# The end of the GIN layer: transpose mode for the features, and six PSUM buffers in turn

## The chip, the cores and the metric

The kernel runs on one core of a Trainium2 chip. A core has TensorE (matrix products, written to the accumulation memory PSUM), VectorE, ScalarE and GpSimd, and SyncE, which here only starts transfers. Each engine works through its own queue of instructions in order and waits at semaphores for the others. In the profile they are PE (and PEld for its weight loads), DVE, ACT, POOL and SP. The metric is the device time of one execution in microseconds (us).

## The reference

The reference is a stack of four graph layers over 3125 nodes with 128 features and 100,000 edges. Each layer is added to its input and the sum is normalised over the features of each node:

```python
x = _layernorm(x + _L0_gnn_ref(...), axis=-1)   # three GCN layers
x = _layernorm(x + _L1_gnn_ref(...), axis=-1)   # linear, summed over edges
x = _layernorm(x + _L2_gnn_ref(...), axis=-1)   # GIN
x = _layernorm(x + _L3_gnn_ref(...), axis=-1)   # two relational layers, 8 relations
```

The third, GIN, is the one that matters here:

```python
out = (1.0 + eps) * x + aggr
h = jax.nn.relu(_batchnorm(out @ W1 + b1, g1, beta1))
h = jax.nn.relu(_batchnorm(h @ W2 + b2, g2, beta2))
```

The batch normalisation needs the mean and variance of a feature over all nodes; the layer normalisation that follows needs those of a node over all features.

## The kernel before, in words

**Tiling.** The nodes are 25 blocks of 128 (`NB`), `xa` holds the current features in SBUF with nodes on the partitions, 128 x 25 x 128 float32. Most loops go over `CH`, seven chunks of 4, 3, 4, 3, 4, 3 and 4 blocks. The kernel first turns the edge list into dense adjacency blocks and per-relation count blocks (up to line 468), then runs GCN (`product`), the second layer and GIN (`product_t`), then the relational layers.

**The end of GIN.** `linear` and `batchnorm_relu` work with features on the partitions, because the batch statistics run over nodes. So their result `y2` lies transposed. The last loop of that part (lines 702 to 708) goes over the chunks. For each block it lets TensorE multiply `y2` by the identity `ident`, which transposes it into PSUM (line 706), and adds the residual by multiplying the identity with `xa` into the same PSUM columns (line 707). `normalise` with `shared=True` then takes the layer norm of a chunk out of PSUM: statistics per block on DVE (lines 123 and 124), a square root on ACT (126), reciprocal and the negated scaled mean on DVE (127, 130), and the scaling itself, even blocks on ACT (134) and odd blocks on DVE (137), written back into `xa`.

**Buffers.** The PSUM pool `f_ps` has three tags, `mi`, `acc` and `bld`, with two buffers each, and the loop takes `bld`. In this stretch of the program the other two serve earlier parts of GIN: `acc` the edge sums, `mi` the output of `linear`.

**What follows.** `x3` is `xa` under another name. A new SBUF pool `f_rel` reuses the memory of the pool in which `y2` lay, and a new PSUM pool `f_psr` reuses all of `f_ps`. Line 718 loads a weight matrix; `split2` (735 on ACT, 736 on DVE) splits `x3` in two parts for the relation product; `store3` (744 and 746 on ACT, 745 and 747 on DVE) splits it in three bfloat16 parts in a tile `t` with two buffers, and line 748 stores each chunk to the DRAM table `xt_d` through SP's queue. The relation product (`relation`) loads count blocks as bytes (758, SP's queue, six buffers), casts them on ACT (766) or DVE (768) into three buffers and multiplies (771), ten matmuls to a cast. The remaining blocks of nodes are not dense: `gathered` lets POOL gather rows of `xt_d` (805), DVE builds one-hot matrices (797), and TensorE multiplies (813). POOL cannot start before all of `xt_d` is stored. `linear1` then transposes `x3` (845), copies it (846), and applies the weights.

**What sets the order.** The kernel is written without semaphores; a scheduler that takes the program, its data dependences and the pools' buffers fixes the order of each engine's queue when the kernel is built. Instructions of a later part can therefore stand ahead of those of an earlier one, and the order can change where only a buffer name was edited.

Of the kernel before, what the change touches and what calls it, by code (L numbers as in the profile page):

```python
# [8 lines left out]
F32 = mybir.dt.float32  # L9
# [12 lines left out]
P = 128  # L22
# [23 lines left out]
def cols(m0, nb):  # L46
    return slice(m0 * P, (m0 + nb) * P)
# [7 lines left out]
CH = ((0, 4), (4, 3), (7, 4), (11, 3), (14, 4), (18, 3), (21, 4))  # L55
# [17 lines left out]
def listed(ctx: ExitStack, tc: tile.TileContext, p: dict, out: bass.AP, bad):  # L73


    nc = tc.nc
# [4 lines left out]
    ident = const.tile([P, P], F32, name="ident")  # L81
# [36 lines left out]
    def normalise(y, v, nb, shared=False):  # L118

        st = small.tile([P, 4, 6], F32, name="st")  # L120
        mv = small.tile([P, 4, 2], F32, name="mv")
        for i in range(nb):
            nc.vector.bn_stats(st[:, i, :], v[:, i, :])
            nc.vector.bn_aggr(mv[:, i, :], st[:, i, :])
        rs = small.tile([P, 4], F32, name="rs")
        nc.scalar.activation(rs[:, :nb], mv[:, :nb, 1], AF.Sqrt, bias=eps_ln, scale=1.0)
        nc.vector.reciprocal(rs[:, :nb], rs[:, :nb])
        if shared:
            ng = small.tile([P, 4], F32, name="ng")
            nc.vector.scalar_tensor_tensor(ng[:, :nb], mv[:, :nb, 0], -1.0, rs[:, :nb],  # L130
                                           op0=OP.mult, op1=OP.mult)
        for i in range(nb):
            if shared and i % 2 == 0:
                nc.scalar.activation(y[:, i, :], v[:, i, :], AF.Identity, bias=ng[:, i : i + 1],
                                     scale=rs[:, i : i + 1])
                continue
            nc.vector.tensor_scalar(
                y[:, i, :], v[:, i, :], mv[:, i, 0:1], rs[:, i : i + 1],
                op0=OP.subtract, op1=OP.mult,
            )  # L140
# [4 lines left out]
    def blocks(ap):  # L145
        return ap.rearrange("p (b c) -> p b c", c=P)

    with ExitStack() as lists, tc.tile_pool(name="f_ps", bufs=1, space=PSUM) as psum:
# [17 lines left out]
        with tc.tile_pool(name="f_t1", bufs=1) as t1:  # L166
# [24 lines left out]
            t = psum.tile([P, 512], F32, name="mi", tag="mi", bufs=2)  # L191
# [114 lines left out]
            for g in range(2):  # L306
                t = psum.tile([P, 512], F32, name="mi", tag="mi", bufs=2)
# [23 lines left out]
            t = psum.tile([P, 512], F32, name="mi", tag="mi", bufs=2)  # L331
# [5 lines left out]
            t = psum.tile([P, 512], F32, name="mi", tag="mi", bufs=2)  # L337
# [132 lines left out]
        with ExitStack() as stage:  # L470
# [165 lines left out]
            t = psum.tile([P, 512], F32, name="mi", tag="mi", bufs=2)  # L636
# [40 lines left out]
            def batchnorm_relu(y, i):  # L677

                _, g, beta = c2[i]
                ends = [(a, min(a + 512, N)) for a in range(0, N, 512)]  # L680
                st = small.tile([P, len(ends), 6], F32, name="bst")
                for j, (a, b) in enumerate(ends):
                    nc.vector.bn_stats(st[:, j, :], y[:, a:b])
                mv = small.tile([P, 2], F32, name="bmv")
                nc.vector.bn_aggr(mv, st)
                s = small.tile([P, 2], F32, name="bsc")
                nc.scalar.activation(s[:, 0:1], mv[:, 1:2], AF.Sqrt, bias=eps_ln, scale=1.0)
                nc.vector.reciprocal(s[:, 0:1], s[:, 0:1])
                nc.vector.tensor_mul(s[:, 0:1], s[:, 0:1], g)
                nc.vector.tensor_mul(s[:, 1:2], mv[:, 0:1], s[:, 0:1])  # L690
                nc.vector.tensor_sub(s[:, 1:2], beta, s[:, 1:2])
                for m0, nb in CH:
                    c = cols(m0, nb)
                    nc.scalar.activation(y[:, c], y[:, c], AF.Relu, bias=s[:, 1:2], scale=s[:, 0:1])
# [3 lines left out]
            y2 = nd.tile([P, NP], F32, name="y2", tag="halves", bufs=2)  # L698
            for m0, nb in CH:
                linear(y2, 1, y1[:, cols(m0, nb)], m0, nb)  # L700
            batchnorm_relu(y2, 1)
            for m0, nb in CH:
                t = psum.tile([P, 512], F32, name="bld", tag="bld", bufs=2)
                for i in range(nb):
                    o = t[:, cols(i, 1)]
                    nc.tensor.matmul(o, y2[:, cols(m0 + i, 1)], ident, start=True, stop=False)
                    nc.tensor.matmul(o, ident, xa[:, m0 + i, :], start=False, stop=True)
                normalise(xa[:, m0 : m0 + nb, :], blocks(t), nb, True)

# [4 lines left out]
    with tc.tile_pool(name="f_rel", bufs=1) as rp, tc.tile_pool(  # L714
        name="f_psr", bufs=1, space=PSUM
# [36 lines left out]
        def relation(r, m0, nb, pieces, work, rate, casts):  # L752

            acc = psum.tile([P, 512], F32, name="acc", tag="acc", bufs=2)
            w = nb * P
            for g in range(5):
                m8 = rp.tile([P, 4, 5, P], U8, name="m8", bufs=6)
                nc.sync.dma_start(
                    m8[:, :nb].rearrange("p b k d -> p b (k d)"),
                    rel[r][m0 : m0 + nb, :, 5 * g : 5 * g + 5].rearrange("b p k d -> p b (k d)"),  # L760
                )
                m = rp.tile([P, 5, 4 * P + 8], F32R, name="m", bufs=3)
                v = m[:, :, :w].rearrange("p k (b d) -> p k b d", d=P)
                src = m8[:, :nb].rearrange("p b k d -> p k b d")
                if casts[g]:
                    nc.scalar.copy(v, src)  # L766
                else:
                    nc.vector.tensor_copy(v, src)  # L768
                for k in range(5):
                    for i, x in enumerate(pieces):  # L770
                        nc.tensor.matmul(  # L771
                            acc[:, :w], x[:, 5 * g + k, :],
                            m[:, k, :w],
                            start=(g == 0 and k == 0 and i == 0), stop=(g == 4 and k == 4 and i == 1),
                        )
                ahead[0] += rate
                while ahead[0] >= 1.0:
                    next(work, None)
                    ahead[0] -= 1.0
            return acc[:, :w]  # L780
# [42 lines left out]
        with tc.tile_pool(name="f_z", bufs=1) as zp:  # L823
# [57 lines left out]
            for m0, nb in DENSE:  # L881
                z = zp.tile([P, R, 512], F32, name="z", bufs=2)
                for r in range(R):
                    inv = load_inv(r, m0, nb)
                    acc = relation(r, m0, nb, xs, work, 2.2, (0, 1, 0, 1, 0))
# [5 lines left out]
        with tc.tile_pool(name="f_hr", bufs=1) as hp:  # L891
# [15 lines left out]
            for m0, nb in CH:  # L907
                o = psum.tile([P, 512], F32, name="mi", tag="mi", bufs=2)
                for a in range(2):
                    nc.tensor.matmul(o[:, : nb * P], root2[:, a, :], hT[:, a, cols(m0, nb)],  # L910
                                     start=(a == 0), stop=(a == 1))
# [28 lines left out]
            for r in range(R):  # L940
                nxt = None
                for i, (m0, nb) in enumerate(DENSE):
                    inv = load_inv(r, m0, nb)
                    acc = relation(r, m0, nb, hr, work, 2.2, (1, 1, 1, 1, 1))
# [3 lines left out]
                    c = cols(m0, nb)  # L948
# [586 lines left out]
@with_exitstack  # L1535
def gnn_kernel(ctx: ExitStack, tc: tile.TileContext, p: dict, out: bass.AP):
    bad = ctx.enter_context(tc.tile_pool(name="flag", bufs=1)).tile([P, 1], I32, name="bad")
    listed(tc, p, out, bad)
    rv = tc.nc.values_load(bad[0:1, 0:1], min_val=0, max_val=1)
    with tc.If(rv > 0):  # L1540
        general(tc, p, out)
# [32 lines left out]
```

## Time and profile before

| | before |
|---|---|
| median of 3 runs | 2251.15 us (2241.75 to 2253.26) |
| the profiled execution, its own time | 2257.92 us |
| its span, first to last instruction | 2256.1 us |
| mean granted TensorE clock | 0.921 |
| busy: PE / DVE / ACT / POOL | 1932.3 / 1271.3 / 1058.1 / 903.2 us |
| line 706, first and last start | 943.5 to 968.1 us |
| first matmul of the relation product (771) | 977.1 us |
| first gather of the relation stage (805) | 1006.6 us |

A busy share is an average over stages with different limits. The changed loop takes up some 25 us of the span, so the views to read are those of that window: what each engine waits for there, and when the work that follows begins. The clock is the share of full speed that TensorE was granted. A line such as `[2.85 <-DVE xa L137]` at the end of a row says that the engine stood idle for 2.85 us before it, until DVE's work on line 137 released it.

### The profile page before, as it was taken

To read this page: it belongs to the slowest core of one execution; us is meant where nothing else is said; L and a number is where in the kernel's file an instruction comes from. 1 tells how busy PE (TensorE), PEld (TensorE's weight loads), DVE (VectorE), ACT (ScalarE), POOL (GpSimd) and SP (SyncE) were. 2 spreads that over 40 slices of the span, in tenths; PEclk is the share of its full clock that TensorE was granted. 3 is DMA by queue.
4 is the path that set the end of the run, shared out by engine and by line. 5 is a ranking of instruction groups with operands and counts; after the bars stand their busy time and mean duration, and the time that the engine had idled before them with its cause. 6 is when DMAs were issued, how large, how long until landed. Compare 5 with 4: busy or idle time off the path is not lost.

```text
span 2256.1 us, 31992 instructions
## 1 busy us (share of the span) xinstructions
PE 1932.3 (86%) x12201; PEld 1394.4 (62%) x12201; DVE 1271.3 (56%) x2303; ACT 1058.1 (47%) x1151; POOL 903.2 (40%) x898
## 2 busy tenths in 40 slices
PE   1667769999999699778998999999878899888984
PEld 1445536666665588555776667567536777767763
DVE  4888889999996563363443445344236434334423
ACT  1666644544442465541231333232227667666761
POOL 3222121121120000017747357437524766666664
PEclk9776679999999899888998999999989999999996
DMA  3444466788787788075655567456538877777762
GB/s 91 182 175 165 178 194 210 264 291 271 261 270 244 244 262 243 20 206 137 192 155 160 155 179 204 129 157 180 140 102 256 231 207 226 208 215 225 209 172 71
DMA packets 384636, 433.06 MB, mean 192 GB/s; under 512 B 28731, under 2 KB 350301, under 8 KB 384472
## 3 DMA queue, kind: packets, MB, share of 16 engines
q1 hardware_dynamic: 314318, 278.95, 40.3%
q0 software_dynamic: 45920, 119.66, 17.9%
q10 hardware_dynamic: 24234, 32.31, 5.0%
q8 instruction: 97, 1.59, 0.3%
q14 instruction: 67, 0.55, 0.1%
HBM read 319.22 MB, written 111.58 MB: 191 GB/s over the span
## 4 chain that ended last, share of the span: by engine, by line
PE 59%; DVE 17%; issue 7%; DMA 7%; ACT 4%; POOL 3%; another core or an unknown queue 2%; ACTq 0%; DVEq 0%; SPq 0%; POOLq 0%
PE acc L771 25%; PE ga L813 8%; PE acc L534 7%; PE acc L569 6%; PE mi L861 4%; PE mi L851 4%; DMA g<-dsf,irow 3%; DVE lo L161 2%; DVE rhq L161 2%; PE bld L448 2%; ACT m L766 2%; DVE hi L161 2%; DVE rlo L161 1%; POOL gx L805 1%
## 5 line engine op out<-in xcount | busy, mean ns | idle before, releaser
L771 PE MATMUL acc<-m,hilo 128*128 128x384 f32 (+1 forms) x3200 | 780.2, 387 | 50.5 <-issue 35.3
L771 PEld LDWEIGHTS acc<-m,hilo 128*128 128x128 f32 x3200 | 582.1, 195 | 139.6 <-issue 62.0
L766 ACT CAST m<-m 128x2560 fp32r<-128x2560 uint8 (+1 forms) x224 | 455.4, 2061 | 449.4 <-PE ga L813 121.9
L805 POOL DMA_INDIRECT gx<-xt_d,gsrc x355 | 391.3, 1102 | 566.0 <-DMA inv<-inv_d 306.5
L805 POOL DMA_INDIRECT gx<-ht_d,gsrc x355 | 362.5, 1021 | 220.5 <-issue 79.3
L534 PE MATMUL acc<-m,parts 128*128 128x512 bf16 (+1 forms) x1575 | 334.6, 359 | 11.6 <-DMA r_L_gnn_g<-in_L_gnn_g 10.5
L813 PE MATMUL ga<-oh,gx 128*128 128x192 bf16 (+1 forms) x2442 | 266.4, 246 | 63.4 <-issue 35.3
L813 PEld LDWEIGHTS <-gx 128*128 128x128 bf16 x2442 | 178.6, 100 | 157.2 <-issue 124.7
L797 DVE TENSOR_TENSOR oh<-iota,gkey 128x768 bf16<-128x768 bf16 (+1 forms) x188 | 100.1, 533 | 270.6 <-PE ga L813 128.0
L534 PEld LDWEIGHTS <-parts 128*128 128x128 bf16 x1575 | 152.9, 98 | 135.5 <-issue 13.9
L768 DVE CAST m<-m 128x2560 fp32r<-128x2560 uint8 (+1 forms) x96 | 152.0, 1584 | 115.6 <-issue 36.4
L455 ACT CAST rb<-bld 128x800 uint16<-128x800 f32 x179 | 143.7, 828 | 125.8 <-PE bld L448 120.7
L462 POOL DMA_DIRECT2D rel<-rb x112 | 64.4, 583 | 286.9 <-ACT rb L455 182.8
L569 PE MATMUL acc<-mf,halves 128*128 128x512 f32 (+1 forms) x700 | 154.2, 378 | 18.0 <-ACT mf L566 17.8
L569 PEld LDWEIGHTS acc<-mf,halves 128*128 128x128 f32 x700 | 128.0, 190 | 38.3 <-issue 18.7
L161 DVE TENSOR_TENSOR lo<-iota,kT 128x2048 bf16<-128x2048 bf16 x100 | 122.0, 1220 | 1.5 <-PE bld L271 1.5
L271 PE MATMUL bld<-hi,lo 128*128 128x50 bf16 x1600 | 75.8, 202 | 41.1 <-DVE hi L161 25.9
L566 ACT CAST mf<-m 128x2560 fp32r<-128x2560 bf16 (+1 forms) x42 | 88.2, 2102 | 48.1 <-PE acc L569 38.6
L448 PE MATMUL bld<-rhq,rlo 128*128 128x200 bf16 x896 | 107.7, 253 | 1.7 <-DVE rb L457 1.0
L745 DVE TENSOR_TENSOR e<-mi,t 128x512 f32<-128x512 f32 x50 | 34.3, 687 | 129.9 <-ACT t L744 125.7
L271 PEld LDWEIGHTS <-lo 128*128 128x128 bf16 x1600 | 64.9, 108 | 66.5 <-DVE hi L161 25.8
L448 PEld LDWEIGHTS <-rlo 128*128 128x128 bf16 x896 | 82.9, 98 | 36.5 <-issue 8.3
(216 smaller groups left out, 2137.2 us busy)
## 6 DMA issues: line engine op xcount, KB each, us to landing
m<-rel SPq DMA_DIRECT2D x160, 320.0 KB
rel<-rb POOLq DMA_DIRECT2D x112, 400.0 KB
m<-adj SPq DMA_DIRECT2D x60, 640.0 KB
m<-rel SPq DMA_DIRECT2D x160, 240.0 KB
m<-adj_t SPq DMA_DIRECT2D x40, 640.0 KB
m<-adj SPq DMA_DIRECT2D x45, 480.0 KB
adj_t<-at SPq DMA_DIRECT2D x25, 800.0 KB
adj<-av SPq DMA_DIRECT2D x25, 800.0 KB
```

Of the source, the lines that this page charges most:

```text
L161: nc.vector.tensor_tensor(o, (iota2 if of is None else of)[:, None, :width, :].to_broadcast([P, PU // 2, width, 2]), k[:, :, None, :].to_b ...
L271: nc.tensor.matmul(pt[:, j, : 2 * NB], lo[:, j // 2, :, j % 2], hi[:, j // 2, :, j % 2], start=True, stop=True)
L448: nc.tensor.matmul(pt[:, k, : R * NB], lo[:, j // 2, :, j % 2], hq[:, j // 2, :, j % 2], start=True, stop=True)
L455: nc.scalar.copy(o, src)
L534: nc.tensor.matmul(o, x[:, k, :], m(k - k0), start=(k == 0 and i == 0), stop=(k == NB - 1 and i == 2))
L569: nc.tensor.matmul(acc[:, :w], x[:, 5 * g + k, :], mf[:, k, :w], start=(g == 0 and k == 0 and i == 0), stop=(more is None and g == 4 and k ...
L766: nc.scalar.copy(v, src)
L768: nc.vector.tensor_copy(v, src)
L771: nc.tensor.matmul(acc[:, :w], x[:, 5 * g + k, :], m[:, k, :w], start=(g == 0 and k == 0 and i == 0), stop=(g == 4 and k == 4 and i == 1),)
L797: nc.vector.tensor_tensor(oh[:, : nt // 2], iota2[:, None, : GW * R, :].to_broadcast([P, nt // 2, GW * R, 2]), gkey[:, g, t : t + nt].rear ...
L805: nc.gpsimd.indirect_dma_start(out=gx.rearrange("p i c -> p (i c)"), out_offset=None, in_=table[:], in_offset=bass.IndirectOffsetOnAxis(ap ...
L813: nc.tensor.matmul(acc[:, a:z], gx[:, i, :], oh[:, t % 4 // 2, a - c0 : z - c0, t % 2], start=(a // 512 not in seen), stop=(t == GT[g] - 1 ...
```

## The change

The seven chunks take their PSUM tile from the tags `bld`, `mi` and `acc` in turn, each with two buffers, where all took `bld`. The product of `y2` with the identity is issued in TensorE's transpose mode, `is_transpose=True`; the addition of the residual remains an ordinary matmul that accumulates on it.

```diff
-            for m0, nb in CH:
-                t = psum.tile([P, 512], F32, name="bld", tag="bld", bufs=2)
+            for c, (m0, nb) in enumerate(CH):
+                bank = ("bld", "mi", "acc")[c % 3]
+                t = psum.tile([P, 512], F32, name=bank, tag=bank, bufs=2)
                 for i in range(nb):
                     o = t[:, cols(i, 1)]
-                    nc.tensor.matmul(o, y2[:, cols(m0 + i, 1)], ident, start=True, stop=False)
+                    nc.tensor.matmul(o, y2[:, cols(m0 + i, 1)], ident, start=True, stop=False, is_transpose=True)
                     nc.tensor.matmul(o, ident, xa[:, m0 + i, :], start=False, stop=True)
                 normalise(xa[:, m0 : m0 + nb, :], blocks(t), nb, True)
```

In the program as built, TensorE issues the chunks in the same order as before. In the queues of DVE, ACT and SP the instructions of neighbouring chunks and of the parts that follow are interleaved differently: on ACT, line 718's load and two of line 744's copies stand between the scalings of chunks 2 and 3 and those after, and the first four transposes of line 845 with their copy (846) stand ahead of the relation product's first matmul; before, they stood at the start of `linear1`, behind the products of the first chunk.

## The prediction

> **What bounds the kernel now.** I read the table by stretches first (its columns are us, then busy us and count for PE, its weight loads, DVE, ACT and POOL, then granted clock, DMA share, GB/s). From 943 to 977 us, where the changed loop lies, nothing is near full, and POOL has not begun:
>
> ```profile
> 943.00:977.00 34.00, 16.93 (x100) 16.06 (x100) 19.83 (x87) 18.39 (x39) 0.00 (x0) 0.71 0.24 65
> 977.00:1010.00 33.00, 30.11 (x120) 23.87 (x120) 23.64 (x25) 18.16 (x17) 2.84 (x3) 0.93 0.87 260
> 1010.00:1100.00 90.00, 76.45 (x412) 55.27 (x413) 31.44 (x30) 18.65 (x8) 66.10 (x62) 0.87 0.58 156
> ```
>
> So this is a chain of waits. The view of the tile `bld` names both sides, TensorE waiting for the last reader of a buffer and VectorE waiting for the last matmul of a chunk:
>
> ```profile
> L706 PE MATMUL bld<-ident,y x50: 274/304/582, 943.5 to 968.1; 128*128 128x128 f32 x50
>   DVE xa L137: 20.1, 10
>   PE bld L707: 9.7, 4
> ```
>
> The timeline shows the turn-taking. Two chunks fill both buffers, TensorE stops until L137 has read the first, and VectorE then stops until it is refilled:
>
> ```profile
> 951.33 0.80 PE L706 MATMUL bld<-ident,y 128*128 128x128 f32 x2 [2.85 <-DVE xa L137]
> 954.76 0.50 DVE L123 BATCH_NORM_STATS2 st<-bld 128x6 f32<-128x128 f32 x2 [3.13 <-PE bld L707]
> 961.01 0.50 DVE L123 BATCH_NORM_STATS2 st<-bld 128x6 f32<-128x128 f32 x2 [1.79 <-PE bld L707]
> 968.62 0.17 DVE L833 MEMSET hT<- 128x128 f32 x1 [3.16 <-PE bld L706]
> 977.07 30.11 PE L771 MATMUL acc<-m,hilo 128*128 128x512 f32 x120 [8.11 <-issue]
> 1006.55 1.04 POOL L805 DMA_INDIRECT gx<-xt_d,gsrc  x1 [306.55 <-DMA inv<-inv_d]
> 1010.33 0.43 PE L813 MATMUL ga<-oh,gx 128*128 128x192 bf16 x3 [3.15 <-DMA gx<-xt_d,gsrc]
> ```
>
> The last three lines are the stage's two exits. TensorE begins the relation product at 977.07. POOL's first gather starts at 1006.55, after the last of seven xt_d stores was issued at 1002.58. TensorE finishes its 120 matmuls and waits 3.15 us for that gather. In order of time the chain holds the xt_d stores from 977.59, then gathers to about 1027, then mostly TensorE. Downstream is therefore as early as these two exits are.
>
> **What the Trainium skill says.** "TensorE: Matmul & The Clock Gate", section Terms, calls transpose mode 4 times faster for FP32. The trace shows two: L706 leaves 50 matmul records for 25 blocks, while the existing transposes of L845 leave 25 for 25 and four start 0.44 us after one another's begin, 0.11 us each, one pass. The trace decides. Its section Part 4: PE-mode transpose says transposes do not count as busy for the clock gate in the same way; no run shows that yet. "PSUM — Partial Sum Buffer", The four PSUM rules, says that an fp32 transpose sets the bits that let the next matmul add, so L707 can go on adding. Its section on bank collisions says that two engines must not touch one bank at once. The trace agrees: within a chunk L134 (0.46 us) and L137 (0.41) alternate, the next starting 0.03 to 0.10 us after the other's end.
>
> **Transposes.** Before, a block costs four passes: 0.85 us in slow clock (944.72 to 945.57), 0.445 warm (959.36 to 959.81), so 0.213 and 0.111 a pass. After, three. Removed: 25 passes, 2.8 us warm to 5.4 cold. With two buffers only the first chunk of each of four turns is on the path: 4 passes each, three cold and one warm, 3 x 0.85 + 0.44 = 3.0 us.
>
> **Six buffers.** In the built order TensorE issues chunks 0 to 5 without a buffer wait, and chunk 6 waits for chunk 0's readers. From 943.46, cold until about 947.0 as before, 16.6 passes fit; the other 46.4 of 63 take 5.2 us: 952.2. Chunk 0's last L137 ends near 951.2 by the walk below, so chunk 6 runs 952.2 to 953.6 (before: 965.2 to 968.6).
>
> VectorE is then the stage's engine. The first statistics start at 943.46 + 12 x 0.213 + 0.15 = 946.2 (946.88 before). From there its queue holds, by start-to-start times of before: 25 statistics and aggregates, 0.19 + 0.09, 7.0; seven times L127 and L130, 1.1; eleven L137 at 0.34, 3.7; and ahead of the first relation cast L833, two L745, six L736 and two L747, 5.4; the cast itself 1.76. Sum 19.0. Walking both queues in the built order leaves 1.8 us of waiting, mostly the sqrt round trips: cast done 967.0, against a relation start of 977.07: **10.0 us**. The cross-check is the waits that go: 3.13 + 1.79 + 3.16 + 0.40, plus 0.7 earlier start and a 0.5 us one-hot moved behind, 9.7.
>
> **What moves with it.** The order changes on ACT, too. L718's DMA, which waits for chunk 6's last L706 because it reuses that memory, now stands ahead of the scaling of chunks 3 to 6. Behind it hang L134, L126, then VectorE's L137. By the walk ACT gets there at 954.2, TensorE is done at 953.5: 0.7 us of cover. SP's relation loads are freed by the same L706: 968.60 becomes about 953.6. Before, the six loads took 969.5 to 976.9 at about 1.05 us each, the first done about 3.1 after issue; after, first done 956.7, needed at 965.2, so hidden by 8.5 us. Load 6 waits for load 1's semaphore, 956.7, hidden. The four L845 transposes and the x3t copy (0.6 us ACT) go ahead of the relation product; ACT waits for a store there anyway. That takes 0.44 us from TensorE near 1120.
>
> The gather's start must be followed through stores. Two `t` buffers make each pair of stores wait for the pair before. Before: issues 977.59, 987.22, 994.84, 1002.58; landings 5.4, 3.9, 4.9, about 4. After: the first L747 ends 964.8, store 0 lands near 968.9 (no seventh load ahead); L744/745 to 970.4; the ACT cast 970.5 to 972.9, L746 to 973.4; the VectorE cast (TensorE's second group done 972.7) to 974.5, L747: store 2 at 975.1. Landing 979.0, ACT's cast to 980.0, L744, L745, cast to 983.5, L747: store 4 at 984.2. Landing 988.5, L744 to L747, SP passing load 17 at 989.3: store 6 at 991.5. Landing 4: gather near 995.4, **11.1 us** earlier than 1006.55. TensorE's 120 matmuls end near 997.2 and the first gathered data come 3.8 after the gather: resume 999.2 against 1010.33, 11.1. POOL gathers one tile per 1.25 us and idled until then, so nothing holds it back.
>
> Sum: 11.1 + 0.4 = **11.5 us**. The profiled execution took 2257.92 us (span 2256.1, 1.8 around it): 2246.4, ratio 0.9949. On the median 2251.15: **2239.7**.
>
> **Unknown ends.** A transposing pass cannot be below nothing; if it still takes two passes, the same walk gives a cast end of 969.1, 2.1 us lost. The clock: if transposes keep TensorE cold throughout, chunk 5 ends at 956.9, chunk 6 at 959.5, L718 blocks ACT for 5.3 us, cast done 972.2: a gain near 5 to 7 us. I take warm-up as before, since two of three passes stay ordinary matmuls.
>
> **Rivals.** (1) Cold TensorE, as just priced: about 2245. For it: that section of the skill, and a loop already at 0.71 clock; against: no idle turn of 2.9 us is left before chunk 6. (2) The store chain eats the gain: every other store sits on SP behind relation loads that wait for casts that wait for TensorE groups. If landings stay at 5.4 us and casts slip between each pair, 2 to 3 us a pair, the gather gains 2 to 4 us: about 2249. For it: the landing was 5.43 with loads ahead; against: TensorE's groups are 10 us earlier themselves. (3) It ends slower: the relation stages get a lower clock. TensorE holds 59% of the chain, some 1330 us, at mean clock 0.921; each 0.01 costs about 14.5 us. It cancels the gain at 0.913 and passes +0.5% at 0.905: about 2263. For it: the windows from 1010 on already vary from 0.87 to 1.00 and the three times spread over 11.5 us; against: the work there is the same. (4) The change does not do what it says, buffers still in turn of two: only 3.0 us, 2248; against: the built order shows no buffer wait before chunk 6.
>
> **Chances and range.** Half a percent, 11.3 us, is about what a measurement of this kernel can tell from no change, and my sum lies on it. Full carry-through 0.62 (about two thirds of it above 11.3, counting 3 us of unmodelled shorter waits on the gather up to 1027); cold 0.12, nearly all within, a tenth above by spread; stores 0.09 and (4) 0.04, within; slower clock 0.13, most of it past +0.5%. That is faster 0.45, same 0.44, slower 0.11. The stretch 1007 to 1027 holds about 8 us of TensorE idle under the gather, so errors of the first case lean to more gain; I move 0.05 to faster. The range takes the cold and store ends with the runs' own spread: 2229 to 2255; the likeliest case alone 2231 to 2246.
>
> **What would show it.** L706 with 25 records; no wait on L137 but at chunk 6; VectorE's idle under `bld` near 4 us instead of 9.7; relation product at 966 to 968; gather at 994 to 997; L718 not waiting past 954.5. Wrong if the clock in the loop stays near 0.5, ACT stands at L718, the store issues are not about 10 us earlier, or the clock after 1010 changes the total.

## The result, and the profile after

The change makes the kernel faster by two thirds of a percent: 2233.12 us median of 6 executions (2229.74 to 2234.57) against 2248.19 us (2241.75 to 2253.26) for the kernel before, a ratio of 0.9933 with a 95% interval of 0.9911 to 0.9954. The forecast was 2239.7 us, a ratio of 0.9949, in a range of 2229 to 2255. Two later timings of the same kernel gave 0.9931 (0.9905 to 0.9956) and 0.9953 (0.9939 to 0.9967); the forecast lies in all three intervals.

The line numbers after 702 are one higher in the changed kernel: 706 and 707 become 707 and 708, 771 becomes 772, 805 becomes 806. Its profiled execution took 2231.44 us with a span of 2229.5, and reached the changed loop 8.8 us sooner, at 934.63 us in place of 943.46, though nothing before the loop had changed. Two executions of the kernel before differ by as much as 6.7 us at that place, so times below are counted from TensorE's first matmul of the loop, and the 8.8 us are taken as scatter. These first matmuls, before and changed:

```profile
943.46 0.49 PE L706 MATMUL bld<-ident,y 128*128 128x128 f32 x2 [4.01 <-ACT y L694]
934.63 0.33 PE L707 MATMUL bld<-ident,y 128*128 128x128 f32 x1 [4.01 <-ACT y L694]
```

The table by stretches of the changed kernel, with the stretches moved by 8.8 us to match those of before (columns as there):

```profile
934.20:968.20 34.00, 22.00 (x116) 19.26 (x117) 27.33 (x98) 23.88 (x46) 0.00 (x0) 0.75 0.54 154
968.20:1001.20 33.00, 26.98 (x123) 20.00 (x122) 15.60 (x16) 12.38 (x10) 11.29 (x12) 0.95 0.72 207
1001.20:1091.20 90.00, 79.58 (x444) 60.05 (x443) 36.96 (x35) 23.34 (x10) 67.39 (x60) 0.91 0.62 166
```

VectorE's 19.8 busy us of the first stretch are now 27.3, with work that used to come later, and POOL has its first 12 instructions in the second stretch in place of 3. The view of the tile `bld` of the changed kernel:

```profile
L707 PE MATMUL bld<-ident,y x11: 272/273/421, 934.6 to 944.3; 128*128 128x128 f32 x11
  PE bld L708: 4.0, 2
```

The other 14 transposes are in `mi` and `acc`, 25 records in all in place of 50. The 20.1 us that the view of before gives for L137 count TensorE's matmuls (8.6) and their weight loads (9.1) apart, and 2.4 us of ScalarE; for TensorE they are three waits of 2.85 us. These are gone: the only wait left in the loop is the first, for the input (4.01 us, on line 694). The timeline of the changed kernel, the lines that answer to those of before:

```profile
937.08 0.49 DVE L123 BATCH_NORM_STATS2 st<-bld 128x6 f32<-128x128 f32 x2 [3.41 <-PE bld L708]
938.86 0.30 DVE L123 BATCH_NORM_STATS2 st<-mi 128x6 f32<-128x128 f32 x1 [0.68 <-PE mi L708]
940.19 0.30 DVE L123 BATCH_NORM_STATS2 st<-acc 128x6 f32<-128x128 f32 x1 [0.21 <-PE acc L708]
957.46 30.38 PE L772 MATMUL acc<-m,hilo 128*128 128x512 f32 x120 [1.56 <-DVE m L769]
986.56 1.05 POOL L806 DMA_INDIRECT gx<-xt_d,gsrc  x1 [293.54 <-DMA inv<-inv_d]
991.01 0.43 PE L814 MATMUL ga<-oh,gx 128*128 128x192 bf16 x3 [3.18 <-DMA gx<-xt_d,gsrc]
```

VectorE waits 0.68 and 0.21 us for chunks 1 and 2, then never again for TensorE. What releases the relation product is now VectorE's cast (L769), no longer the last L137. The product starts 957.46 - 934.63 = 22.8 us after the loop's start, where it was 33.6, and the gather 51.9, where it was 63.1. TensorE's wait for the gather did not change, 3.18 us after 3.15.

### The profile page after: what moved, and what is told of

It reads as the page before. It is cut to its first block, busy times and chain, and to the rows that moved or that the text cites. A ratio compares the mean times of both kernels' runs of the same rounds, so it can differ in the third digit from the quotient of the medians.

```text
span 2229.5 us, 31941 instructions
## 1 busy us (share of the span) xinstructions
PE 1911.2 (86%) x12176; PEld 1382.8 (62%) x12176; DVE 1269.3 (57%) x2303; ACT 1056.7 (47%) x1151; POOL 900.9 (40%) x898
## 4 chain that ended last, share of the span: by engine, by line
PE 58%; DVE 17%; DMA 8%; issue 7%; ACT 4%; another core or an unknown queue 3%; POOL 2%; ACTq 0%; SPq 0%; DVEq 0%; POOLq 0%
PE acc L772 24%; PE ga L814 7%; PE acc L534 7%; PE acc L569 6%; PE mi L852 4%; PE mi L862 3%; DVE lo L161 2%; DMA g<-dsf,irow 2%; PE bld L448 2%; DVE rhq L161 2%; ACT m L767 2%; DVE hi L161 2%; DVE rlo L161 1%; DMA back<-ht_d 1%
## 5 line engine op out<-in xcount | busy, mean ns | idle before, releaser
L772 PEld LDWEIGHTS acc<-m,hilo 128*128 128x128 f32 x3200 | 580.4, 194 | 132.3 <-issue 53.1
L534 PE MATMUL acc<-m,parts 128*128 128x512 bf16 (+1 forms) x1575 | 333.7, 358 | 11.6 <-DMA r_L_gnn_g<-in_L_gnn_g 10.5
L769 DVE CAST m<-m 128x2560 fp32r<-128x2560 uint8 (+1 forms) x96 | 151.9, 1584 | 115.8 <-PE ga L814 32.2
```

The costliest lines, as they stand in the source:

```text
L534: nc.tensor.matmul(o, x[:, k, :], m(k - k0), start=(k == 0 and i == 0), stop=(k == NB - 1 and i == 2))
L772: nc.tensor.matmul(acc[:, :w], x[:, 5 * g + k, :], m[:, k, :w], start=(g == 0 and k == 0 and i == 0), stop=(g == 4 and k == 4 and i == 1),)
```

## The experiments

The theory: two buffers made TensorE and VectorE take turns; six let VectorE set the pace; the time won there moves both exits, the relation product and the gather, and is carried to the end unchanged. The rivals: transpose mode is the larger part; the later stages add a gain of their own; only one exit counts. Two of the chips here run the kernel before in some 2155 us and the others in some 2249, so a run is compared with the kernel before on its own chip. On the two faster chips the kernel before was timed but not profiled; the early-turn kernel, which ran on one of them and has the loop of the kernel before, stands in for it there. The table has, for each kernel's profiled execution, us from the loop's first matmul, read from the start times of the relation product, the first gather and the span's end, and the ratio of times with its interval.

| kernel | relation product | first gather | end | ratio to before |
|---|---|---|---|---|
| before | 33.6 | 63.1 | 1312.7 | |
| before again | 33.6 | 63.4 | 1316.1 | 1.000 (0.998 to 1.002) |
| changed | 22.8 | 51.9 | 1294.9 | 0.9933 (0.9911 to 0.9954) |
| changed, third | 22.8 | 53.1 | 1305.8 | 0.9953 (0.9939 to 0.9967) |
| four loop buffers | 22.9 | 51.7 | 1300.4 | 0.9959 (0.9933 to 0.9985) |
| scaling on ScalarE | 18.6 | 55.5 | 1303.1 | 0.9954 (0.9937 to 0.9971) |
| four store buffers | 24.1 | 42.8 | 1290.2 | 0.9911 (0.9882 to 0.9940) |
| four store buffers again | 25.1 | 44.1 | 1287.5 | 0.9896 (0.9866 to 0.9927) |
| four store buffers, scaling on ScalarE | 18.8 | 46.4 | 1290.1 | 0.9894 (0.9861 to 0.9927) |
| *on the chips of 2155 us:* | | | | |
| early turn only | 34.4 | 65.3 | 1216.7 | 1.0006 (0.9994 to 1.0019) |
| transpose only | 34.1 | 64.2 | 1211.2 | 0.9989 (0.9975 to 1.0004) |
| transpose, kept busy | 31.0 | 61.1 | 1214.6 | 0.9989 (0.9977 to 1.0001) |
| buffers only | 25.6 | 52.2 | 1204.9 | 0.9944 (0.9924 to 0.9965) |
| changed, again | 22.8 | 52.9 | 1206.4 | 0.9931 (0.9905 to 0.9956) |

**Transpose mode alone.**

```diff
-                bank = ("bld", "mi", "acc")[c % 3]
+                bank = "bld"
```

> Transpose mode alone, all seven chunks in the two bld buffers as before. If the loop is bound by the turns of TensorE and VectorE (my theory), only the first chunk of each of four turns is on the path: 3.0 us in the loop, from TensorE's first transposing matmul to the first matmul of the relation product 30.6 us in place of 33.6, ratio near 0.9987. If TensorE's passes set the loop, all 25 passes count, 2.8 to 5.4 us, and the waits on L137 (20.1 us) shrink. Rival on the stages after it: the transposes of x3 stay where they were before, so if their early place makes the later gain, this kernel keeps none of that part.

Measured: 0.9989, an interval that holds 1, and the loop was not shortened at all, 34.1 us where 30.6 was forecast. The windows of the loop's four turns, first of the kernel before, then of this one (columns as above; the granted clock is the third number from the end; this kernel's first window opens 0.7 us before its first matmul):

```profile
943.40:951.33 7.93, 5.02 (x28) 4.83 (x28) 3.52 (x21) 5.69 (x12) 0.00 (x0) 0.75 0.01 2
951.33:958.92 7.59, 4.73 (x28) 4.54 (x29) 3.82 (x22) 2.28 (x6) 0.00 (x0) 0.81 0.00 0
958.92:965.17 6.25, 3.39 (x29) 3.21 (x29) 3.82 (x22) 2.28 (x6) 0.00 (x0) 0.94 0.00 0
965.17:977.10 11.93, 3.82 (x17) 3.55 (x17) 8.77 (x25) 7.84 (x15) 0.00 (x0) 0.50 0.67 185
```

```profile
937.50:945.85 8.35, 4.19 (x21) 4.00 (x22) 3.70 (x21) 6.79 (x13) 0.00 (x0) 0.76 0.00 0
945.85:953.19 7.34, 3.85 (x21) 3.66 (x21) 3.69 (x21) 2.20 (x6) 0.00 (x0) 0.73 0.01 2
953.19:961.43 8.24, 4.74 (x22) 4.45 (x22) 3.77 (x21) 2.20 (x6) 0.00 (x0) 0.50 0.00 0
961.43:972.40 10.97, 2.86 (x13) 2.59 (x13) 8.48 (x24) 7.39 (x14) 0.00 (x0) 0.50 0.73 200
```

The third turn has a quarter fewer passes and takes longer, 8.24 us in place of 6.25, at a clock of 0.50 where the kernel before had 0.94. The two kernels were profiled on chips of different speed, but that is not the reason: the early-turn kernel, on the same chip as this one, has the third turn of the kernel before:

```profile
953.84:960.09 6.25, 3.39 (x29) 3.20 (x29) 3.81 (x22) 2.28 (x6) 0.00 (x0) 0.94 0.00 0
```

The waits for a buffer grew as well, from 2.85 to 3.43 and 3.49 us, and end with ScalarE's L134 in place of VectorE's L137, since the order of scaling differs. Two causes were open, the clock and these waits, and the next kernel tells them apart.

**Transpose mode with TensorE kept busy.** On top of the edit above, it computes something more: nine products that nothing reads.

```diff
                     nc.tensor.matmul(o, ident, xa[:, m0 + i, :], start=False, stop=True)
+                if c % 2 == 1:
+                    idle = psum.tile([P, 512], F32, name="mi", tag="mi", bufs=2)
+                    for _ in range(3):
+                        nc.tensor.matmul(idle, ident, y2[:, : 4 * P], start=True, stop=True)
                 normalise(xa[:, m0 : m0 + nb, :], blocks(t), nb, True)
```

> Transpose mode with the two bld buffers, and nine products of 512 columns that nothing reads, put where TensorE waits for a buffer: four behind the first turn, five behind the second. ScalarE's and VectorE's queues stand as in transpose mode alone, which kept the loop at 34.1 us with its third turn at half clock (0.64 us a block). If the lower clock took the saving away, the third turn runs at 0.33 us a block and is 1.2 us shorter at least in what VectorE waits for, loop 32 to 33 us. If it was the longer wait for the scaling in the new order, the loop stays at 34 us although the clock is up.

Its windows over the same four turns (the first opens 0.8 us before the first matmul), and the wait before its fourth turn:

```profile
937.40:945.85 8.45, 7.61 (x29) 5.36 (x29) 3.71 (x21) 6.91 (x13) 0.00 (x0) 0.80 0.01 2
945.85:952.53 6.68, 6.68 (x32) 4.24 (x32) 3.66 (x21) 2.20 (x6) 0.00 (x0) 1.00 0.00 0
952.53:958.52 5.99, 2.50 (x23) 2.30 (x22) 3.66 (x21) 2.20 (x6) 0.00 (x0) 1.00 0.00 0
958.52:969.30 10.78, 2.66 (x13) 2.40 (x13) 8.47 (x24) 7.37 (x14) 0.00 (x0) 0.51 0.73 203
958.52 0.33 PE L707 MATMUL bld<-ident,y 128*128 128x128 f32 x1 [3.49 <-ACT xa L134]
```

With useless work added, the third turn runs at full clock and takes 5.99 us, and the loop 31.0 us in place of 34.1, more than the 32 to 33 expected. The queues of VectorE, ScalarE and SyncE hold the same instructions in the same order, and the wait of 3.49 us is still there before the fourth turn, so the lower clock had taken the saving. What lowered it is less sure: each of the two kernels was profiled once, and no run separates the fewer passes, the longer gap and transpose mode itself. In the total 3 us are near the limit of what was measured: the ratio is 0.9989 again.

**Buffers alone.**

```diff
-                    nc.tensor.matmul(o, y2[:, cols(m0 + i, 1)], ident, start=True, stop=False, is_transpose=True)
+                    nc.tensor.matmul(o, y2[:, cols(m0 + i, 1)], ident, start=True, stop=False)
```

> Six buffers in turn alone, the features multiplied by the identity in the ordinary mode. My theory: VectorE sets the loop as soon as the buffers let TensorE run ahead; four passes a block in place of three delay the first statistics and the last L706 by some 1 us each, cast done 2.1 us later than in the full change: loop to relation product near 25 us in place of 33.6, gain 8 to 9 us plus what the stages after it add, ratio near 0.996. If transpose mode were the larger part: less than 4 us.

```profile
938.74 0.49 PE L707 MATMUL bld<-ident,y 128*128 128x128 f32 x2 [4.01 <-ACT y L694]
964.31 27.26 PE L772 MATMUL acc<-m,hilo 128*128 128x512 f32 x105 [12.51 <-issue]
990.97 1.43 POOL L806 DMA_INDIRECT gx<-xt_d,gsrc  x1 [295.92 <-DMA m<-rel]
```

Measured: 25.6 us (964.31 - 938.74), close to the 25 expected, and a ratio of 0.9944. The buffers bring most of the change. Transpose mode then takes 2.8 us more off the start of the relation product (22.8), but not off the gather: 52.2 us with the buffers alone, 51.9 to 53.1 with both. In the totals the two can't be told apart (2144.39 and 2141.95 us on one chip).

**Four buffers in the loop.**

```diff
-                bank = ("bld", "mi", "acc")[c % 3]
+                bank = ("bld", "mi")[c % 2]
```

> Transpose mode with four buffers, bld and mi in turn. My theory: VectorE is the loop's engine once TensorE can run ahead by two chunks, so TensorE waits some 1 us for chunk 4's buffer and nothing is lost: 23 to 24 us to the relation product (22.9 with six), ratio 0.993 to 0.9945. If six are needed: waits on L137 of 3 us or more come back and the relation product is at 26 us or later.

Measured: TensorE waits on L137 again, 0.96 and 0.94 us, and nothing behind it notices: 22.9 us and 51.7 us. Four buffers are enough here. The ratio, 0.9959, lies above the 0.993 to 0.9945 expected, but its interval (0.9933 to 0.9985) overlaps all three of the changed kernel.

**The early transposes alone.** The kernel before, with the transposes of the first chunk of `x3` and their copy written ahead of the relation product, which gives the stores the paired order of the changed kernel.

```diff
-            def linear1(z, m0, nb):
-                w = min(nb * P, HL - m0 * P)
+            def turned(m0, nb):
                 x3t = zp.tile([P, 512], F32, name="x3t", bufs=1)
                 t = psum.tile([P, 512], F32, name="mi", tag="mi", bufs=2)
                 for i in range(nb):
                     nc.tensor.transpose(t[:, cols(i, 1)], x3[:, m0 + i, :], ident)
                 nc.scalar.copy(x3t[:, : nb * P], t[:, : nb * P])
+                return x3t
+
+            head = turned(*CH[0])
+
+            def linear1(z, m0, nb):
+                w = min(nb * P, HL - m0 * P)
+                x3t = turned(m0, nb) if m0 else head
```

> The kernel before, with one of the change's side effects alone: the transposes of the first chunk of x3 and their copy stand ahead of the relation product; GIN's end is as before. Plain shift: 0.44 us from TensorE, ratio 0.9990 to 1.0005. Rival: the changed order of stores and casts that comes with it (xt_d stores in pairs) is worth 3 us or more, ratio 0.9985 or less, with the first gather 1 us or more earlier relative to the first relation matmul.

Measured: 1.0006 (0.9994 to 1.0019), and the gather came later after the relation product, not earlier: 30.9 us in place of 29.5. This side effect is worth nothing that can be measured; the 0.4 us of the sum are neither confirmed nor refuted.

**The two kernels again.** Both without an edit.

> The kernel before once more, timed against itself and profiled on the chip of the others. Ratio 1.000, and from TensorE's first matmul in the loop 33.6 us to the relation product, 63 us to the first gather, 1205 to 1220 us to the end if the chip is like that of the runs before it. What differs is the scatter that the comparison of any two profiles carries.

> The changed kernel once more, for a second execution with a profile and a time on the chip of the others. Theory of a plain shift: 10.8 us at the first relation matmul and 11.2 at the first gather stay 11 to 12 us to the end, and the 17.7 us that the first pair of profiles shows from the loop to the end is partly scatter of one execution (expect 10 to 14 here). Rival: the later 3 to 7 us come again at the same places (200 gathers on, and in the second relational layer), 16 to 18 us from the loop to the end. Ratio 0.993 to 0.995 in both.

> The changed kernel once more, beside the two that follow on the same chip. Plain shift: 23 us from the loop's first matmul to the relation product, 52 to 53 to the first gather; from the first gather to the end the same as the kernel before within 5 us. Ratio 0.993 to 0.995.

The places in the loop come again to within 0.1 us for the relation product and 1.2 us for the gather. The later stretch does not. From the first gather to the end, the kernel before takes 1312.7 - 63.1 = 1249.6 and 1252.7 us; the changed one 1243.0 and 1305.8 - 53.1 = 1252.7. On the faster chip the changed kernel takes 1153.5, the early-turn kernel, which is like the one before, 1151.4. So the 17.7 us from the loop to the end that the first two profiles differ by hold some 6 of scatter, and no later stage has been shown to add a gain. The third timing's ratio, 0.9953, fell just outside the 0.993 to 0.995 expected of it.

**Scaling on ScalarE.** This takes VectorE's 11 L137 off the loop.

```diff
-            if shared and i % 2 == 0:
+            if shared:
```

> The changed kernel with all the scaling of this loop on ScalarE (25 L134 in place of 14, no L137 in the loop). My theory, VectorE sets the loop: 11 x 0.34 = 3.7 us leave it and the turns within a bank go, ScalarE takes 11 x 0.35 = 3.9 more of its own 24 us: relation product 2 to 3 us earlier (20 to 21 us after the loop's first matmul), ratio near 0.992. If ScalarE is as near its limit: no change or 1 to 2 us later.

Measured: the relation product starts 4.2 us earlier, more than the 2 to 3 expected. That fits a loop that VectorE paces, but the edit also ends the turns of the two engines within a bank, and no run tells these two apart. The gather starts 2.4 to 3.6 us later than in the changed kernel, and the ratio, 0.9954 where 0.992 was expected, is no better. Moving one exit forward and the other back gained nothing.

**Four buffers for the stored split.**

```diff
-            t = rp.tile([P, 4, 3, D], BF, name="t3", bufs=2)
+            t = rp.tile([P, 4, 3, D], BF, name="t3", bufs=4)
```

> The changed kernel with four buffers in place of two for the three-part split that is stored to xt_d, so that no pair of stores waits for the pair before. My theory says that the first gather, not the first relation matmul, decides what the rest gets: then the gather starts 8 us or more earlier (about 44 us after the loop's first matmul in place of 52), TensorE's wait for it goes, and 4 to 8 us come on top of the full change, ratio against before near 0.990. Rival, the relation product's start decides: the casts stand behind the stores' splits on both engines, it starts 1 to 2 us later, and the total is that of the full change or 1 us more.

> Four buffers for the stored split, once more. If the first gather decides: gather at 43 us after the loop's first matmul, relation product at 24, and 4 us or more less than the changed kernel on the same chip (ratio 0.990 to 0.992). If the 4 us of the first time were scatter: within 2 us of the changed kernel.

SP's queue, first of the changed kernel, then of the second profile of this one (start, length, count of transfers; only the stores' lines are shown, the loads between them left out):

```profile
955.34 1.06 SPq L749 DMA_DIRECT2D xt_d<-t  x2
967.05 0.91 SPq L749 DMA_DIRECT2D xt_d<-t  x2
975.69 1.78 SPq L749 DMA_DIRECT2D xt_d<-t  x2
982.78 0.36 SPq L749 DMA_DIRECT2D xt_d<-t  x1
```

```profile
958.20 1.19 SPq L749 DMA_DIRECT2D xt_d<-t  x2
962.92 0.91 SPq L749 DMA_DIRECT2D xt_d<-t  x2
968.49 0.36 SPq L749 DMA_DIRECT2D xt_d<-t  x1
972.15 0.45 SPq L749 DMA_DIRECT2D xt_d<-t  x1
975.01 0.36 SPq L749 DMA_DIRECT2D xt_d<-t  x1
```

The same profile's first matmul of the loop, relation product and first gather:

```profile
936.67 0.47 PE L707 MATMUL bld<-ident,y 128*128 128x128 f32 x1 [4.01 <-ACT y L694]
961.75 4.42 PE L772 MATMUL acc<-m,hilo 128*128 128x512 f32 x10 [2.02 <-DVE m L769]
980.77 1.05 POOL L806 DMA_INDIRECT gx<-xt_d,gsrc  x1 [288.12 <-DMA inv<-inv_d]
```

From the first store to the last, 27.4 us became 16.8. The gather starts at 42.8 and 44.1 us, the relation product 1.3 and 2.3 us later than in the changed kernel, and the kernel is faster: 2226.29 us against 2237.43 for the changed one on the same chip, and the two intervals of the ratio to before do not touch (0.9866 to 0.9927, 0.9939 to 0.9967). This version beats both kernels, and the exit that counts, by all that was measured, is the gather. The table shows it: on the slower chips the nine profiles take 1243 to 1253 us from the first gather to the end, a spread of 10 us, but 1262 to 1284 us, a spread of 22, from the relation product. The traces show it early in that stretch. The 50th of 355 gathers starts 134.6 and 134.9 us after the loop's first matmul in the two profiles of the kernel before, 123.5 and 125.1 in the changed kernel, 125.7 with the scaling on ScalarE, 114.6 and 116.6 here: what the gather won is still there, and the earlier product of the kernel with the scaling on ScalarE is not.

Two things keep this from being a test of the gather alone. The built order also differs: TensorE's queue has the first gathered products behind 70 relation matmuls, not 120, and TensorE's wait for the first gather, expected to go, is 3.13 us as before. And the tile `t` serves the later stores to `ht_d` too; but as the time from the gather to the end, 1247.4 and 1243.4 us, is within that of the other kernels, no gain from these is seen.

> Four buffers for the stored split and all scaling of this loop on ScalarE. With six buffers for the loop alone the scaling on ScalarE brought the relation product 4.2 us forward and the gather 3.6 us back, because ScalarE also serves the stored split. If the gather decides, this is no better than four store buffers alone: gather at 43 to 46 us, relation product at 20, ratio 0.990 to 0.993. If both exits count alike: 2 us or more below it, ratio 0.989.

With the scaling on ScalarE added to it (both edits above), the relation product starts 6.3 us earlier again, the gather 2.3 us later (46.4), and the total stays, 2226.87 us. That fits the same reading but does not prove it: the intervals of the two ratios (0.9861 to 0.9927, 0.9866 to 0.9927) are wider than what is to be told apart.

## Why the prediction was right, point by point

**Six buffers** was right in its mechanism and nearly in its size. Predicted from the loop's first matmul, and measured: first statistics 2.7 and 2.45 us; chunk 6 begins at 8.7 and 8.7; relation loads issued at 10.1 and 10.0; cast done 23.5 and 22.8; so 10.0 us were forecast for the relation product and 10.8 came. VectorE's idle time under TensorE was to be near 4 us and is 3.41 + 0.68 + 0.21 = 4.3.

**What moves with it** held. L719's load stands ahead of the scaling and cost nothing: ACT came to it at 10.2 us, when L707's last pass was just done, and the copy behind it waited 0.12 us. The chain of stores was forecast at 21.4, 31.6, 40.7 and 48.0 us and measured at 20.7, 32.4, 41.1 and 48.2; the gather at 51.9 and 51.9, 11.1 us and 11.2. TensorE resumed at 56.4 where 55.7 was forecast, 10.5 us earlier in place of 11.1.

**Transposes** is the step that failed, in its claim for two buffers: "3 x 0.85 + 0.44 = 3.0 us" took the clock of each turn as given. The third turn lost it, and nothing was left. With TensorE kept busy the loop takes 31.0 us, 2.6 less than the 33.6 of the kernel before, and that with a clock of 1.00 in the second turn where the kernel before had 0.81; so the 3.0 us are near in size, but no run shows them at an equal clock. In the changed kernel this did not matter, as TensorE runs its loop through without a pause; there the transposes took 2.8 us off the start of the relation product, where the walk had 2.1. The statement of the Trainium skill, "TensorE: Matmul & The Clock Gate", Part 4: PE-mode transpose, that transposes do not count as busy for the clock gate in the same way, which carried rival 1, did not decide here: with a third of the passes in transpose mode the loop went from 0.213 to 0.111 us a pass some 4 us after its start, as before. No run had transposes alone.

**The sum** added 0.4 us for the early transposes, for which no run shows a gain. And the prediction did not say which of the two exits counts: both were forecast to come 10 to 11 us earlier, so the result could not show it. There was luck in that. The later kernels speak for the gather: product starts 4 and 6 us earlier, with the gather 2 to 4 us later, brought no total that could be told from the one without, and a gather about 9 us earlier, with the product 1 to 2 us later, took 11 us off. The sum was right because it followed the gather. Its 11.5 us compare with 15.1 (10.3 to 20.0 by the interval), 14.9 and, the narrowest, 10.6 us by the ratio's 0.0047 (7.4 to 13.7).

**The rivals.** Cold TensorE, the store chain and buffers still in turn of two are excluded by the profile. A lower clock did not come, 0.928 against 0.921. The reason given for leaning to more gain, shorter waits on the gather, was wrong: the first wait was 3.18 us, and 4.47 in the third profile, and in 20 us from just behind the gather's start, TensorE was busy for 12.60 us before and for 12.19 and 12.01 after.

## What to carry to other kernels

Follow a local gain to every exit of its stage, and ask which of them the next stage waits for longest; here a chain of stores through two buffers, not the product on TensorE, seems to have decided, and two more buffers there were worth as much as the whole change. Where two engines take turns, add buffers until the slower one hardly waits; here six did no more than four. In a loop bound by such turns, shortening TensorE's part can cost it its clock and give the saving back; look at the clock of each turn.

## What was not expected of the hardware

Less work on TensorE went with a longer part of a turn, in the one profile of transpose mode alone: the 7 blocks of the third turn, of three passes, took 0.64 us each at a clock of 0.50, where 7 of four passes had taken 0.445 at 0.94 (0.96 in the second profile of the kernel before). Nine products of 512 columns that nothing reads, in the gaps, brought the blocks to 0.33 us.
